# The first group's first part and the last group's last part as two halves in turn, with three written-out orders of steps

## The chip, the cores and the metric

One kernel runs on one core of a Trainium2 chip. The metric is the device time of one execution in microseconds, as a median of several runs. The core has a matrix engine (TensorE, PE in the profile; PEld is its weight load), a vector engine (VectorE, DVE), an activation engine (ScalarE, ACT), GpSimd (POOL), and SyncE (SP), whose queue issues nearly all transfers here. Each engine takes its own instructions strictly in the order in which the program lists them, and waits on semaphores for what others make.

## The reference

The input x is 64 batches of 256 tokens with 256 features, all in float32. Two layers are applied, each a graph-attention block (gnn) and a feed-forward block (ffn), each behind a layernorm and added to x:

```python
x = x + gnn0(layernorm(x))   # relu(x W1+b); attention without mask; relu(. W2+b); attention with mask
x = x + ffn0(layernorm(x))   # top 127 of 256 tokens go through gelu(. w1 + b1) w2 + b2, scaled
x = x + gnn1(layernorm(x))   # one masked attention
x = x + ffn1(layernorm(x))   # a Mamba-2 block: causal conv of 4 taps, decay matrices per head, gate
def attention(inp, mask, W, a):
    h = inp @ W
    e = leaky_relu((h @ a1)[:, :, None] + (h @ a2)[:, None, :])
    return elu(softmax(where(mask, e, -inf)) @ h)
```

Every batch is worked alone: no number passes from one batch to another.

## The kernel before, in words

The 64 batches are taken in 32 groups of two (`G = 2` at L46). A group is 512 token columns (`T`) or 4 chunks of 128 tokens (`C`). Each group passes three parts, which are Python generators: `first_part` (gnn0, L489 to L569), `middle` (ffn0 and gnn1, L571 to L724) and `last` (ffn1, L726 to L932, then the store at L972). A `yield` ends a step, and a step is a handful of instructions. First part has 55 steps, middle 57, last 87. Here they are lanes a, b and c; c30.12 is step 12 (from 0) of the last part of group 30.

The order in which all engines get their instructions is written out by hand. `along` (L234) reads the 199 letters of `ORDER` (L22 to L25) again and again; a letter runs one step of its lane, a capital also lets the lane begin its next group. A lane that has nothing to do is skipped. So in the steady round the first part of one group runs beside the middle part of the one or two groups before it and the last part of the group before those. At the beginning b and c have no work, at the end a has none, then b has none. a0 runs alone up to step 54, a1 alone up to step 34 (then b0 begins), and c31, the last part of the last group, runs all of its 87 steps alone.

What the steps do, as far as it matters below:

- a (gnn0): steps 1 and 2 layernorm; 3 and 4 transposes on PE; 5 to 8 the products with `mlp1_w`; 9 to 12 products with `W_fc` and two folded columns; 13 to 16 `scores` (transposes into `fb`, max, leaky relu, exp with sums on ACT, the division on POOL, L446); 17 to 20 the rest of `W_fc`; 21, 22 `turned`; 23 to 34 `u` and the two nested elu (ACT, DVE, ACT, DVE, POOL L541); then `mlp2_w`, `W_hand` and a second attention.
- b (ffn0, gnn1): 3 to 7 the choice of tokens; 8 to 27 four products `ph` with a gelu each; 28 to 35 `py` with `w2`; 36 to 42 the sum, moments and layernorm; 43, 44 the score columns (DVE, `junk` L689); 45 `fb` on PE; 46 to 56 attention.
- c (ffn1): 1 to 4 layernorm, transposes, `pd`; 5, 6 the step sizes and their running sum (`csT`, L753), stored to DRAM and spread back over the partitions by 8 DMAs (`E`, L781), one for each head; 8 to 31 five products `pp` with `W_in` (PE), each with the 4 conv taps (ACT L813, three DVE L817) and a silu (ACT L822, DVE L823), and for four heads `decays` (a minimum on DVE L792, four exp on ACT L798); 32 to 39 transposes `xd`; 40, 41 `pb` and `cb`; 42 to 73 per pair of heads `E * cb` (DVE L870), `pz` and gate, `py`, the sum (DVE L895) and gating (POOL L896); 74 to 86 the norm (`pss`, `pst`, L922) and four `po` with the sum into x, then the store.

Weights are made ready by two more generators: `made_ready_first` (L305) loads what a0 needs and folds the attention vectors into `W_fc` and `W_hand` (DVE, L311 to L318); `made_ready` (L341) loads everything else, folds `W_l1` (also L314), transposes the result (`pa`), halves some weights and multiplies `W_out` with `W_lin`. Its steps are taken in a0 after step 14, its DMAs are in the order of the list `fetches`, with many small ones (`dtb`, `negA`) ahead of the attention vector `a_l1` (L347).

Of the kernel before, what the change touches and what calls it, by code (L numbers as in the profile page):

```python
# [8 lines left out]
F32 = mybir.dt.float32  # L9
# [10 lines left out]
GELU_A = 0.044715  # L20
ORDER = (
    "cAaccbbbbacbaabccccabbcaccbaccabcbcbacbbcaaaccacaabaaaabccccccccacccacccabcabaaccabccccaccccacababcc"  # L22
    "ccbbccccabcccacaccccbcacbcBbcacbacbbacaaacbacbaabcbbacbcbbbcbbccaCbcbbbcabaaacacbacbaabbbcabbbbbccc"
# [4 lines left out]
def kernel(ctx: ExitStack, tc: tile.TileContext, a: dict, out: bass.AP):  # L28
# [16 lines left out]
    G = 2  # L45
    T = G * N  # L46
    C = T // P
# [6 lines left out]
    assert N == 256 and D == 256 and DS == 64 and HD == 64 and B % G == 0  # L54
# [10 lines left out]
    def view(ap, g):  # L65
        return ap[g * G : (g + 1) * G].rearrange("b (h p) d -> p (b h) d", p=P)

    xin = ctx.enter_context(tc.tile_pool(name="xin", bufs=6))
    first_x = xin.tile([P, C, D], F32, tag="xt", name="xt")
    nc.sync.dma_start(first_x, view(x, 0))  # L70
# [39 lines left out]
    neghalf = cons("neghalf", P, C)  # L110
# [64 lines left out]
    W_in = rows("W_in", a["L1_ffn_W_in"])  # L175
    conv_w = cons("conv_w", P, KC, 4)
    fetched((conv_w, a["L1_ffn_conv_w"].rearrange("(k p) t -> p k t", p=P)))
    conv_b = column("conv_b", a["L1_ffn_conv_b"])

    dtb = cons("dtb", 32 * G, 1)  # L180
    negA = cons("negA", 32 * G, 1)
    for t, ap in ((dtb, a["L1_ffn_dt_bias"]), (negA, a["L1_ffn_A_log"])):
        fetched(*((t[q * NH : (q + 1) * NH, :], ap.unsqueeze(1)) for q in range(32 * G // NH)))
# [42 lines left out]

    def mm(to, lhsT, rhs, start, stop):
        nc.tensor.matmul(to, lhsT, rhs, start=start, stop=stop)  # L228
# [4 lines left out]

    def along(parts, order, n):  # L234

        at = [0] * len(parts)
        now = [None] * len(parts)  # L240
        while at[-1] < n:
            for letter in order:
                i = "abc".index(letter.lower())
                if at[i] == n:
                    continue
                if now[i] is None:
                    if letter.islower() or not (at[i - 1] > at[i] if i else at[0] - at[-1] < 5):
                        continue
                    now[i] = parts[i](at[i])
                if next(now[i], True):  # L250
                    at[i] += 1
                    now[i] = None
# [8 lines left out]
    def power(to, of, scale, eps):  # L261

        nc.gpsimd.tensor_scalar(to, of, scale, eps, ALU.mult, ALU.add)
        nc.gpsimd.tensor_tensor(to, to, neghalf, ALU.pow)

    def moments(xt, s):

        st = sm(f"st{s}", P, C, 6, bufs=1)
        mv = sm(f"mv{s}", P, C, 2, bufs=2)
        rstd = sm(f"rstd{s}", P, C, bufs=2)  # L270
        for c in range(C):
            nc.vector.bn_stats(st[:, c, :], xt[:, c, :])  # L272
        for c in range(C):
            nc.vector.bn_aggr(mv[:, c, :], st[:, c, :])
        power(rstd, mv[:, :, 1], 1.0, EPS)
        return mv, rstd

    def layernorm(xt, mv, rstd, tag):

        xn = [t512(tag, "xn") for _ in range(G)]  # L280
        for c in range(C):
            if c % 2 == 0:
                yield
            nc.vector.tensor_scalar(
                chunk(xn, c), xt[:, c, :], mv[:, c, 0:1], rstd[:, c : c + 1], ALU.subtract, ALU.mult
            )
        return xn
# [3 lines left out]

    def transposed(xn, take):

        xT = []
        for k in range(KD):
            yield
            pt = psum("pt")
            for c in range(C):
                tr(pt[:, tok(c)], chunk(xn, c)[:, k * P : (k + 1) * P], ident)
            xT.append(take())  # L300
            nc.scalar.copy(xT[k], pt)  # L301
        return xT
# [17 lines left out]
    def made_ready_first():  # L320
# [13 lines left out]
        folded(W_fc, avs, H1, t512("w", "junk"))  # L334
        folded(W_hand, hands, D, t512("w", "junk"))
# [4 lines left out]

    def made_ready():  # L341

        fetch()
# [10 lines left out]
        nc.sync.dma_start(W_lin, a["L1_ffn_W_lin"].rearrange("(k p) n -> p k n", p=P))  # L354
        yield
# [15 lines left out]

        for t in (b1h, conv_w, conv_b, W_in[:, :, :DI]):
            nc.vector.tensor_scalar(t, t, 0.5, None, ALU.mult)
# [21 lines left out]
    def scores(f1, f2, mask, strict, tag):  # L395

        yield  # L400
        fb = psum("fb")
        for c in range(C):
            tr(fb[:, tok(c)], f2(c).to_broadcast([P, P]), ident)
        halves = [slice(h * N, (h + 1) * N) for h in range(2)]
        es = [t512(tag, "e") for b in range(G)]
        rows = [fb[:, b * N : (b + 1) * N] for b in range(G)]
        top = sm("top", P, C)
        if mask is None:
            most = sm("most", P, G)
            nc.vector.tensor_reduce(most, fb.rearrange("p (b j) -> p b j", b=G), AX.X, ALU.max)  # L410
            for c in range(C):
                nc.vector.tensor_scalar(
                    top[:, c : c + 1], most[:, c // 2 : c // 2 + 1], f1(c), -1.0, ALU.add, ALU.mult
                )
        else:
            most = sm("topm", P, C)
            for c in range(C):
                e = es[c // 2][:, halves[c % 2]]
                nc.vector.tensor_tensor_reduce(
                    e, rows[c // 2], mask[:, c % 2, :], 1.0, -3e38, ALU.add, ALU.max, most[:, c : c + 1]  # L420
                )
            for c in range(C):
                nc.vector.tensor_scalar(
                    top[:, c : c + 1], most[:, c : c + 1], f1(c), -1.0, ALU.add, ALU.mult
                )
        yield
        nm = sm("nm", P, C)
        nc.vector.scalar_tensor_tensor(nm, top, ALPHA, top, ALU.mult, ALU.min)  # L428
        den = sm("den", P, C)
        for c in range(C):  # L430
            e = es[c // 2][:, halves[c % 2]]
            nc.scalar.activation(e, rows[c // 2] if mask is None else e, AF.Prelu, bias=f1(c), alpha=ALPHA)  # L432
        yield
        for c in range(C):
            e = es[c // 2][:, halves[c % 2]]
            nc.scalar.activation(e, e, AF.Exp, bias=nm[:, c : c + 1], accum_out=den[:, c : c + 1])  # L436
        yield
        if strict:

            nc.vector.scalar_tensor_tensor(den, nm, 1e30, den, ALU.is_lt, ALU.mult)  # L440
        nc.vector.reciprocal(den, den)
        if strict:
            nc.vector.scalar_tensor_tensor(den, nm, 1e30, den, ALU.is_lt, ALU.mult)
        for c in range(C):
            e = es[c // 2][:, halves[c % 2]]
            nc.gpsimd.tensor_scalar(e, e, den[:, c : c + 1], 1.0, ALU.mult, ALU.mult)  # L446
        return es

    def turned(es, tag):

        res = []
        for e in es:
            yield
            pt = psum("pt")
            for h in range(2):
                for j in range(2):
                    tr(
                        pt[:, j * N + h * P : j * N + (h + 1) * P],
                        e[:, h * N + j * P : h * N + (j + 1) * P], ident,
                    )  # L460
            at = t512(tag, "at")
            nc.scalar.copy(at, pt)  # L462
            res.append(at)
        return res

    def elu2(u):

        w = t512("w", "w")
        nc.scalar.activation(w, u, AF.Exp)
        yield  # L470
        nc.vector.tensor_scalar(w, w, 1.0, None, ALU.min)
        nc.scalar.activation(w, w, AF.Exp, bias=neg1)
        yield
        nc.vector.scalar_tensor_tensor(w, w, -1.0, u, ALU.add, ALU.max)  # L474
        return w

    def project(xT, w, tag):

        res = []
        for c in range(C):  # L480
            yield
            pp = psum("pp")
            for k in range(KD):
                mm(pp[:, : D + 2], xT(k, c), w[:, k, :], start=(k == 0), stop=(k == KD - 1))
            h = tiled(t2, (P, D + 2), tag, "hp", 4)
            nc.scalar.copy(h, pp[:, : D + 2])
            res.append(h)
        return res

    def aggregate(at, h, i):  # L490

        u = psum("u")
        for half in range(2):
            for j in range(2):
                mm(
                    u[:, half * D : (half + 1) * D],
                    at[i][:, j * N + half * P : j * N + (half + 1) * P],
                    h[2 * i + j][:, :D],
                    start=(j == 0), stop=(j == 1),
                )  # L500
        return u
# [69 lines left out]
    def ffn0(xt, of):  # L571
# [17 lines left out]
        for c in range(C):  # L589
            b, h = c // 2, c % 2  # L590
            if c == 2:
                yield
# [418 lines left out]
```

## Time and profile before

| | |
|---|---|
| time, median of 3 runs | 3716.49 us (3714.97 to 3717.17) |
| the profiled execution's own time | 3714.94 us |
| its span from the first to the last instruction | 3713.2 us |
| PE busy | 3546.0 us (95%) |
| DVE busy | 2843.1 us (77%) |
| ACT busy | 2170.8 us (58%) |
| POOL busy | 1084.3 us (29%) |
| mean granted TensorE clock | 0.982 |
| store of group 0 issued | 363.64 us |
| stores of groups 27, 28, 29, 30, 31 issued | 3330.49, 3440.34, 3540.87, 3625.36, 3709.05 us |

The stores are one steady round, 109.85 us, apart up to group 28. Busy time is an average over stages with different limits; the table by windows below splits it. In such a table each row is a stretch of the span, followed by its length and the busy time and count of each engine, the granted clock of TensorE (PEclk), and the share and rate of DMA. A table of waits tells which engine's instruction waited for what, in total, how often, and the longest.

### The profile page before, as it was taken

To read this page: it belongs to the slowest core of one execution; us is meant where nothing else is said; L and a number is where in the kernel's file an instruction comes from. 1 tells how busy PE (TensorE), PEld (TensorE's weight loads), DVE (VectorE), ACT (ScalarE), POOL (GpSimd) and SP (SyncE) were. 2 spreads that over 40 slices of the span, in tenths; PEclk is the share of its full clock that TensorE was granted. 3 is DMA by queue.
4 is the path that set the end of the run, shared out by engine and by line. 5 is a ranking of instruction groups with operands and counts; after the bars stand their busy time and mean duration, and the time that the engine had idled before them with its cause. 6 is when DMAs were issued, how large, how long until landed. Compare 5 with 4: busy or idle time off the path is not lost.

```text
span 3713.2 us, 50288 instructions
## 1 busy us (share of the span) xinstructions
PE 3546.0 (95%) x16924; PEld 2545.1 (69%) x16924; DVE 2843.1 (77%) x7209; ACT 2170.8 (58%) x4901; POOL 1084.3 (29%) x1261
## 2 busy tenths in 40 slices
PE   6899999999999999999999999999999999999775
PEld 4567677777767777767777776776776777776553
DVE  3467877778788778787777788877878777778875
ACT  3456565566566556656656656656666655665443
POOL 1123222233332233332223333223333223332221
PEclk8899999999999999999999999999999999999887
DMA  3000111110111111011111011111001111101111
GB/s 114 1 33 16 42 48 48 39 48 15 42 48 48 39 48 38 25 42 48 48 39 48 15 42 48 48 39 48 30 33 42 48 44 43 48 15 37 42 42 47
DMA packets 89074, 150.87 MB, mean 41 GB/s; under 512 B 12144, under 2 KB 55024, under 8 KB 88816
## 3 DMA queue, kind: packets, MB, share of 16 engines
q1 hardware_dynamic: 88816, 147.65, 12.2%
q8 instruction: 135, 2.21, 0.2%
q14 instruction: 123, 1.01, 0.1%
HBM read 125.86 MB, written 17.56 MB: 39 GB/s over the span
## 4 chain that ended last, share of the span: by engine, by line
PE 69%; DVE 16%; ACT 9%; issue 3%; POOL 2%; DMA 1%; SPq 0%; ACTq 0%; POOLq 0%; DVEq 0%
PE pp L228 30%; PE u L228 9%; PE py L228 9%; PE pz L228 6%; PE pt L231 4%; PE pa L228 3%; PE po L228 3%; DVE g L645 3%; ACT e L436 2%; ACT g L646 2%; DVE st L272 1%; ACT e L432 1%; PE fb L231 1%; DVE xt L569 1%; ACT v L637 1%
## 5 line engine op out<-in xcount | busy, mean ns | idle before, releaser
L798 ACT ACTIVATE E<-E,ncs 128x256 f32<-128x256 f32 (+1 forms) x1024 | 381.4, 445 | 159.9 <-DVE E L792 146.9
L446 POOL TENSOR_SCALAR e<-e,den 128x256 f32<-128x256 f32 x384 | 194.6, 523 | 929.0 <-DVE nm L428 415.6
L228 PE MATMUL pp<-W_fc,o 128*128 128x256 f32 (+1 forms) x2048 | 461.2, 380 | 0.0
L228 PEld LDWEIGHTS pp<-W_fc,o 128*128 128x128 f32 x2048 | 383.6, 190 | 67.2 <-issue 15.3
L817 DVE SCALAR_TENSOR_TENSOR xs<-pp,conv_w,xs 128x510 f32<-128x510 f32 (+2 forms) x480 | 357.1, 744 | 54.2 <-ACT xs L813 42.9
L822 ACT ACTIVATE th<-xs 128x512 f32<-128x512 f32 x160 | 100.8, 630 | 357.2 <-DVE xs L817 345.2
L228 PE MATMUL pp<-xT,W_in 128*128 128x512 f32 x640 | 299.9, 601 | 0.0
L541 POOL TENSOR_TENSOR o<-w,o 128x512 f32<-128x512 f32 x128 | 167.5, 1309 | 316.0 <-DVE w L474 316.0
L228 PE MATMUL py<-w,g 128*128 128x256 f32 x1024 | 237.3, 385 | 21.0 <-DVE g L648 21.0
L228 PE MATMUL u<-at,h 128*128 128x256 f32 x1024 | 247.1, 385 | 0.5 <-ACT at L462 0.5
L228 PE MATMUL pp<-o,mlp_w 128*128 128x512 f32 x512 | 238.5, 608 | 5.7 <-POOL o L541 5.7
L228 PE MATMUL pz<-xT,W_in 128*128 128x512 f32 x512 | 243.7, 599 | 0.0
L228 PE MATMUL po<-W_ol,xs 128*128 128x256 f32 x1024 | 243.3, 382 | 0.0
L792 DVE TENSOR_TENSOR E<-E,ccs 128x512 f32<-128x512 f32 x256 | 243.2, 970 | 0.0
L228 PE MATMUL ph<-sel,w 128*128 128x256 f32 x1024 | 242.1, 380 | 0.5 <-ACT sel L615 0.5
L228 PE MATMUL pp<-xT,mlp_w 128*128 128x512 f32 x512 | 241.4, 596 | 0.2 <-ACT xT L301 0.2
L228 PEld LDWEIGHTS py<-w,g 128*128 128x128 f32 x1024 | 191.7, 192 | 70.4 <-DVE g L648 46.3
L870 DVE TENSOR_TENSOR E<-E,cb 128x768 f32<-128x768 f32 x256 | 236.1, 962 | 1.1
L896 POOL TENSOR_TENSOR xs<-xs,gz 128x512 f32<-128x512 f32 x128 | 194.5, 1519 | 132.3 <-DVE xs L895 132.3
L272 DVE BATCH_NORM_STATS2 st<-xt 128x6 f32<-128x256 f32 x512 | 185.2, 414 | 59.0 <-POOL xt L724 32.0
L228 PEld LDWEIGHTS u<-at,h 128*128 128x128 f32 x1024 | 189.8, 190 | 58.7 <-issue 30.7
L679 POOL TENSOR_TENSOR xt<-xn,xt 128x512 f32<-128x512 f32 x64 | 81.2, 1269 | 508.0 <-DVE xn L676 508.0
(178 smaller groups left out, 7666.2 us busy)
## 6 DMA issues: line engine op xcount, KB each, us to landing
E<-csd SPq DMA_DIRECT2D x256, 384.0 KB
xt<-in_x_dram SPq DMA_DIRECT2D x32, 512.0 KB
out_dram<-xt SPq DMA_DIRECT2D x32, 512.0 KB
cs<-xs SPq DMA_DIRECT2D x64, 64.0 KB
w<-in_L_ffn_w_dram SPq DMA_DIRECT2D x2, 1024.0 KB
W_in<-in_L_ffn_W_in_dram SPq DMA_DIRECT2D x1, 1160.0 KB
mlp_w<-in_L_gnn_mlp_w_dram SPq DMA_DIRECT2D x2, 512.0 KB
W_fc<-in_L_gnn_W_fc_dram SPq DMA_DIRECT2D x2, 512.0 KB
```

Of the source, the lines that this page charges most:

```text
L228: nc.tensor.matmul(to, lhsT, rhs, start=start, stop=stop)
L231: nc.tensor.transpose(to, of, eye)
L272: nc.vector.bn_stats(st[:, c, :], xt[:, c, :])
L446: nc.gpsimd.tensor_scalar(e, e, den[:, c : c + 1], 1.0, ALU.mult, ALU.mult)
L541: nc.gpsimd.tensor_tensor(o1[m], w, o1[m], ALU.add)
L645: nc.vector.tensor_tensor(g, g, v, ALU.mult)
L792: nc.vector.tensor_tensor(diag, diag, ccs[:, :, :, h : h + 1].to_broadcast([P, G, 2, P]), ALU.min)
L798: nc.scalar.activation(e[:, b, to], e[:, b, to], AF.Exp, bias=ncs[:, b, half, h : h + 1])
L817: nc.vector.scalar_tensor_tensor(s3[:, :, d:], p3[:, :, : N - d], conv_w[:, m, 3 - d : 4 - d], s3[:, :, d:], ALU.mult, ALU.add)
L822: nc.scalar.activation(th, s, AF.Tanh)
L870: nc.vector.tensor_tensor(e2, e2, cb2, ALU.mult)
L896: nc.gpsimd.tensor_tensor(yt, yt, gz, ALU.mult)
```

## The change

**Sizes.** The functions of the three parts move into a function `sized(G, own)`, made three times: once for groups of two batches, and once for each half of one group (one batch, `G = 1`, 256 token columns). A half has its own instructions on half the columns; tiles that a group has once are shared by the two halves, each using its columns (`wide`, `columns`). For one batch the first part has 42 steps of the same kinds, the last part 78.

**Lanes.** Group 0's first part is lane a (half 0) and lane d (half 1). Group 31's last part is lanes e and f. Lane w makes the weights ready, in 13 steps, with one order of loads: group 1's x now comes ahead of all weights; `a_l1`, `W_out` and `W_lin` come ahead of the small ones (`conv_w`, `dtb`, `negA` and so on). x of group 0 is loaded and the last group stored by halves.

**Orders.** `FIRST` (305 letters) is run once, then `ORDER` (199 letters, a new one) until lane a has done all groups (29 times), then `LAST` (403 letters) once, then the lanes in turn until all is done. Decoded step by step, with the rules of `is_there`:

- `FIRST` begins d0 w0 d1 d2 a0 d3 a1 d4 w1, and the halves go on in turn. a1 (group 1) begins as letter 86, when half 1 has five steps left, and b0 begins as letter 97, at a1.6. At the end of `FIRST` the next steps of the lanes are a3.0, b1.31 and c0.10. The order before passes the same point (there a3.0, b1.31 and c0.11 are next).
- The new round has the same lanes in the same phase as the old, with steps moved by up to some ten places.
- `LAST`: lane b ends its last group just before c30.75 (c30.74 before). e and f may not begin before that, so of their 156 letters only 15 take effect: f does steps 0 to 7 and e 0 to 6 beside c30.76 to c30.86. All the rest of the two halves is run by the closing loop, one step of each in strict turn. Of group 31's middle part only steps 0 to 6 now lie beside c29's end (15 before), and its gelu stage (8 to 27) lies beside c30.4 to c30.25 (before: ahead of c30.7).

Two smaller edits: the row of sums `ss` uses the buffer of `cs` (tag c8) in place of one of four of tag m, and the moments have three buffers in place of two.

```diff
-    first_x = xin.tile([P, C, D], F32, tag="xt", name="xt")
-    nc.sync.dma_start(first_x, view(x, 0))
+    first_x = xin.tile([P, 4, D], F32, tag="xt", name="xt")
+    for half in range(2):
+        nc.sync.dma_start(batch(first_x, half), view(x, 0, half))
...
-    def made_ready_first():
+    def made_ready():
...
-    def made_ready():
-
-        fetch()
+        yield
+        fetch(third_ones - second_ones)
         a_l1 = t512("xd", "a_l1")
...
         nc.sync.dma_start(W_lin, a["L1_ffn_W_lin"].rearrange("(k p) n -> p k n", p=P))
+        fetch()
...
+    def sized(G, own=None):
+        taken = {}
+        def wide(make, tag, *rest):
+            if own is None:
+                return make(tag, *rest)
+            i = taken[tag] = taken.get(tag, -1) + 1
+            if i == len(shared.setdefault(tag, [])):
+                shared[tag].append(make(tag, *rest))
+            return shared[tag][i]
+        def columns(tag, name, most=512):
+            t = wide(lambda tag, name: t512(tag, name) if most == 512 else tiled(t2, (P, most), tag, name, 4), tag, name)
+            return t[:, (own or 0) * N : (own or 0) * N + T]
...
-        ss = t512("m", "ss")
+            ss = columns("c8", "ss")
...
+    both, one = sized(2), [sized(1, half) for half in range(2)]
...
+    def first_half(half):
+        xt = batch(first_x, half)
+        moments = one[half]["moments"](xt, 0)
+        loaded(1)
+        yield from one[half]["gnn0"](xt, moments, lambda: early(1))
+        if at["a"] + at["d"]:
+            of[1, 0] = both["moments"](first_x, 1)
...
+    def last_half(half):
+        xt = batch(xts[n - 1], half)
+        mv, rstd = of[2, n - 1]
+        yield from one[half]["ffn1"](xt, (batch(mv, half), batch(rstd, half)))
+        nc.sync.dma_start(view(out, n - 1, half), xt)
...
+    def is_there(lane):
+        return {
+            "a": at["a"] - at["c"] < 5,
+            "b": at["a"] > at["b"] and at["d"],
+            "c": at["b"] > at["c"],
+        }.get(lane, lane in "dw" or at["b"] == n)
...
     with tc.manual_schedule():
-        along((first_part, middle, last), ORDER, n)
+        for lane in FIRST:
+            step(lane, True)
+        while at["a"] < n:
+            for letter in ORDER:
+                step(letter.lower(), letter.isupper())
+        for lane in LAST:
+            step(lane, True)
+        while any(at[lane] < TIMES[lane] for lane in LANES):
+            for lane in LANES:
+                step(lane, True)
```

## The prediction

> **What bounds the kernel now.** I read the page's 40 slices first, to see where the work is thin.
>
> ```profile
> PE   6899999999999999999999999999999999999775
> ...
> PEclk8899999999999999999999999999999999999887
> ```
>
> PE is full except in the first two slices and the last three. Next the windows, cut where the lanes change: two of the start, the middle, six of the end, one round.
>
> ```profile
> 0.00:101.35 101.35, 59.26 (x229) 41.76 (x229) 34.76 (x140) 30.18 (x65) 15.01 (x30) 0.85 0.34 104
> 101.35:275.70 174.35, 156.40 (x657) 115.01 (x658) 87.67 (x269) 82.92 (x183) 42.02 (x54) 0.94 0.04 12
> ...
> 3457.80:3491.00 33.20, 17.05 (x60) 11.31 (x60) 27.94 (x75) 12.28 (x26) 3.75 (x4) 0.74 0.20 67
> ...
> 3551.70:3584.60 32.90, 17.28 (x57) 10.27 (x56) 26.61 (x63) 12.44 (x24) 3.90 (x5) 0.77 0.23 77
> 3584.60:3616.00 31.40, 29.66 (x149) 18.93 (x149) 27.36 (x49) 18.57 (x46) 10.97 (x10) 0.92 0.08 26
> 3616.00:3633.90 17.90, 11.69 (x58) 8.21 (x56) 6.77 (x20) 3.77 (x6) 4.77 (x5) 0.91 0.09 30
> 3633.90:3692.30 58.40, 32.70 (x111) 16.18 (x110) 37.14 (x51) 21.99 (x48) 4.96 (x3) 0.74 0.18 57
> ...
> 1682.34:1792.17 109.83, 108.94 (x530) 78.65 (x529) 88.04 (x223) 67.51 (x154) 33.77 (x40) 1.00 0.12 40
> ```
>
> A round is PE-bound: 108.94 of 109.83 us. In the start no engine is full; in the end DVE (third pair) and PE take turns. Last, PE's waits, before 276 us and (second fence) after 3457 us.
>
> ```profile
> PE pa L231 <- DVE junk L314: 18.7, 1, 18.7
> PE pt L231 <- DVE xn L284: 14.8, 2, 8.4
> PE pt L231 <- POOL e L446: 6.7, 3, 5.3
> ```
>
> ```profile
> PE pt L231 <- DVE xs L823: 30.2, 6, 6.2
> PE fb L231 <- DVE junk L689: 22.6, 2, 11.4
> ```
>
> Between 276 and 3457 only two are left: py for g (15.4 us, 28 times) and pd for xT (10.0, 29 times), 0.9 us a round.
>
> [...]0.74 and 0.77 in the two stretches with 11 us gaps, 1.00 in the round. [...]424 ns for 256 columns (L689), 691 for 512 (L823); from PSUM 478 (L676), 745 (L895).[...]
>
> **Halving on PE** costs nothing: eight records of 256 columns (u at 3602.35 in the chain) take 1.73 us, four of 512 (pz at 3604.08) 1.72.
>
> **The start**, to the end of FIRST, old 275.7 us. PE's work to there, from the spacing of starts in a round (first part 46, middle 26, last 37, sum 109 as the window has it): three first parts 138, b0 26, 31 steps of b1 12.5, c0's 10 steps 4.5, weights 5: 186. The first product stands at 10.5, so the old loss is 275.7 - 10.5 - 186 = 79.
> - Goes: 18.7. `pa` stood in PE's queue in the middle of a0 and waited for `a_l1`, issued at 34.79 because SP spent 22.4 to 32.3 on dtb and negA, and landed at 44.57. Now it is issued some 12 us earlier, and `pa` (w5) stands behind a0.38, near 60. The small loads are due at w6, in a1.
> - Goes: 6.4 of the 14.8 (a1 waiting behind a0's end; the other 8.4 is the time to the first instruction). b0 fills from a1.6, not from a1.35.
> - New: group 1's 512 KB ahead of the weights, +1.8 us at the 286 GB/s of the first 20 us. `W_fc` and `av` landed at 10.99, and DVE folded to 17.98, 7 us; now near 20, while PE has 6.9 us of mlp1 from some 11 on: 2 lost (0 to 4). Queued behind the fold on DVE: only the scores, due later.
> - Stays: the elu chain. ACT has 8 x 2 x 0.45 (L637: 461 ns) = 7.2 against PE 6.9, and a tail through POOL: 2. The second scores of a and d: chain 5.3, PE's fill 3.5 and 2.7: 5. Clock: 4.
> - From a1 on: old 174.35 for some 139 of work, 35 lost; with b0 beside all of a1 I leave 20 (12 to 30). This is judged, not counted.
>
> Losses 2 + 2 + 5 + 4 + 20 = 33; the phase ends at 10.5 + 186 + 33 = 230: **-45** (-28 to -58).
>
> **The round, 29 times.** Both old waits keep their neighbours. py waits since b26's product (DVE 1697.65) stands behind a54's moments; a54 again stands right before b26, and PE's fill from b28 to c12 is the same. pd and the copy it waits for are one step. New margin: from c46 to c56 (py to py) PE has 2 x 0.44 + 2 x 1.73 + 1.72 = 6.1 us of work (old 7.8); DVE needs 0.75 + 4 x 0.97 + 0.49 = 5.1, hidden with 1.0 left. Before c32, 1.7 us of `junk` moved behind what it needs: safer. `ss` in cs's buffer: cs is read 36 steps earlier; nothing. **0** (-6 to +10: 0.2 a round won, 0.35 lost).
>
> **The end**, from c29.12 (3457.8) to 3713.2, 255.4 us.
> - c29.12 to c29.40, 33.2 with DVE at 84%: the order hardly changes. **-1** (-3 to 0).
> - To c30's store, from c29.74 near 3517, 108. Three pieces. (i) To c30.9, old 34.7: b31's gelu and `py` leave it; the choice's chain and PE work of 18 remain: 22. (ii) Conv, old 32.9: `ph` and `py` come in, PE 20.5 in place of 14.3, while b31's moments and junk leave; DVE has conv 15.2, min 4.6, gelu 6.1, y 0.9 = 26.8, and waits for ACT: 30. (iii) The rest, old 40.4: what left (ii) lands here, DVE 29.8 + 9.6 = 39.4 before the last po, so 42 + 9, less 2 that overlap: 49. Sum 101: **-7** (-15 to +2). The fb wait loses its cost: `fb` now stands behind c30.45, not ahead of the xd transposes.
> - c31's head. From 3625.4 to 3633.9 one chain (xn, pt, pd, dz, csT) runs alone, 8.5 us. As f0 to f7 it lies beside c30's norm and po; its 2.9 us on PE falls partly into waits there (pss, pst: 2.0). What is late next is c30's own po. **-8.5** (-10 to -4). On SP, the halves' four small stores stand ahead of c30's store, which nobody waits for; 12 half E loads in place of 6, some 6 us of issuing, still wait for c30's last py and are due at the first min, over 6 us later.
> - The tail, old 79.3. Conv: the period of one product with a head's decays is 6.58 (3663.26 - 3656.68). In lockstep DVE does 6 taps of 0.52 (pitch 0.785, less 255 x 1.04 ns), twice 0.35 and twice 0.4, 4.6; then it waits for e's exp and f's scaling on ACT, 0.75 + 0.5 and latency, and for tanh: 6.5. **No gain.** E stage: period 7.04 (3683.92 - 3676.88); DVE in halves 5.9 to 6.2, and py of one half hides behind E of the other: 2 x 0.9 and 2 x 0.9 for the later pairs, 3.5. Norm and store: POOL 1.27 to 0.7, sq, pss and ss halved, half a store: 2.5. **-6** (-12 to +4[...]).
>
> Sum -22.5, **-22** (-8 to -38).
>
> **Sum.** -45 + 0 - 22 = -67. The profiled execution took 3714.94 (span 3713.2 and 1.74 around it): 3648. The median of the runs is 1.55 above it: **3649**.
>
> **Rivals.**
> 1. *The ends pack better* (0.17). If DVE reaches 88% in the end, its 174 us there and 9 for halving need 208 of 255, -47; the start could lose 15, not 33. About two thirds of the way, -39 and -57: 3620. For: waits of 11 us in both b/c stretches. Against: in lockstep DVE stands behind ACT.
> 2. *The end gives nothing* (0.20). The halves share tiles; where one half's write must wait for the other's use, lockstep is serial, or the 9.6 us of DVE that land in (iii) cost what the head frees. End 0, start -38: 3678. For: DVE is at 87% in 3584.6 to 3616. Against: each half has its own columns.
> 3. *Slower* (0.05). The py margin: if DVE reaches E late in each round, PE waits in all 29. It decides from 67 / 29 = 2.3 us a round; at 2.9 (DVE 3.9 us later than counted) +84: 3733. For: the margin shrinks by 1.7. Against: no such wait exists now.
> 4. *It doesn't do what it says* (0.03). Shared tiles make the halves serial at both ends and the gaps stay: within 0.2%.
>
> The likeliest case has the remaining 0.55, with 3627 to 3672 as its own range.
>
> **Numbers.** Measurement can tell about 0.2%, 7.4 us, from no change. The range takes in most of 1 and 2: 3612 to 3684. Faster 0.92 (likeliest, 1, 2), same 0.03 (4), slower 0.05 (3).
>
> **What would show it.** PE's wait for L314 is gone. Group 0's store is issued near 319 (363.64 - 45); stores stay 109.85 apart; from c30's store to the end there are 73 us (87.8 - 8.5 - 6); the conv period in the tail is 6.5. I am wrong in the start if group 0's store comes before 306 or after 336, in the round if its period leaves 109.6 to 110.2, in the end if c30's store to the end takes under 66 or over 84.

## The result and the profile after

| | before | after |
|---|---|---|
| median of the runs | 3715.95 us (3714.97 to 3717.17) | 3654.07 us (3652.69 to 3655.5) |
| ratio, 95% interval | | 0.9833 (0.9816 to 0.985) |
| span of the profiled execution | 3713.2 us | 3652.1 us |
| mean granted TensorE clock | 0.982 | 0.990 |
| store of group 0 issued | 363.64 us | 319.89 us |
| stores of groups 28, 30 issued | 3440.34, 3625.36 us | 3392.44, 3586.13 us |

The change takes 61.9 us off the time and 61.1 off the span. The stores split it. Up to group 0's store it is 43.75 us. From there to group 28's it is 4.15 (28 rounds of 109.73 us in place of 109.88). From group 28's store to the end it is 13.2 (259.66 us in place of 272.86).

The page's slices of the kernel after: the first two are now nearly full, and the last three have 8, 7 and 6 tenths in place of 7, 7 and 5.

```profile
PE   8999999999999999999999999999999999999876
...
PEclk9999999999999999999999999999999999999989
```

The windows of after, cut at the same events as those of before in the next fence (columns: stretch, its length, busy us and count of PE, PEld, DVE, ACT, POOL, the granted clock, DMA's share and rate). First the start, up to a1's first transposes, and (after only) from there to the end of `FIRST`. Then two pieces of the last part of group 30: its convolution, from the first `pp` to `pb`, and from there to its last `py`. Then the head of group 31's last part (to its first `pp`), its convolution to the last run of `xd` transposes (the first three stand single before it, one at each new tile), and its E stage to `pss`.

```profile
0.00:66.75 66.75, 53.86 (x233) 42.39 (x233) 31.06 (x132) 30.62 (x76) 15.73 (x35) 0.97 0.51 158
66.75:231.33 164.58, 154.36 (x686) 115.33 (x685) 94.52 (x290) 85.31 (x187) 41.86 (x55) 0.98 0.06 18
...
3491.36:3528.73 37.37, 30.66 (x101) 19.52 (x100) 25.24 (x41) 19.68 (x40) 1.97 (x4) 0.83 0.20 68
3528.73:3564.82 36.09, 26.51 (x126) 15.72 (x125) 29.93 (x72) 14.42 (x37) 12.53 (x12) 0.81 0.06 22
3564.82:3585.59 20.77, 16.86 (x78) 10.53 (x77) 10.93 (x30) 10.16 (x17) 8.42 (x9) 1.00 0.00 1
3585.59:3613.54 27.95, 10.18 (x45) 8.02 (x44) 20.50 (x53) 14.44 (x33) 0.00 (x0) 0.75 0.34 109
3613.54:3637.34 23.80, 20.20 (x118) 14.97 (x118) 22.94 (x48) 11.71 (x34) 4.92 (x6) 0.93 0.10 33
...
```

The same stretches of the kernel before:

```profile
0.00:101.35 101.35, 59.26 (x229) 41.76 (x229) 34.76 (x140) 30.18 (x65) 15.01 (x30) 0.85 0.34 104
...
3551.64:3587.54 35.90, 20.28 (x70) 12.94 (x68) 29.52 (x77) 14.53 (x29) 3.96 (x5) 0.74 0.21 71
3587.54:3612.45 24.91, 24.47 (x130) 15.77 (x129) 22.02 (x30) 15.29 (x40) 8.36 (x8) 0.96 0.09 33
3612.45:3633.91 21.46, 13.94 (x66) 8.76 (x65) 9.20 (x25) 5.03 (x9) 7.38 (x7) 0.92 0.07 25
3633.91:3667.07 33.16, 11.86 (x24) 4.87 (x23) 16.90 (x27) 12.34 (x23) 0.00 (x0) 0.65 0.24 76
3667.07:3694.81 27.74, 22.24 (x101) 12.41 (x101) 21.79 (x26) 11.17 (x27) 5.10 (x3) 0.86 0.10 29
...
```

Read row against row, group 30's convolution has become 1.5 us longer and what follows 11.2. The piece ahead of them (from c29's last `py` on, by the same views 35.70 us before and 24.43 after) gives -11.3, so that together 1.4 are lost. The head gives -0.7; in the changed kernel a product of lane b (`u`, 1.99 us) now stands behind c30's last `py`, and so in the head. The tail's convolution gives -5.2, its E stage -3.9, and norm and store, which come last (18.39 and 14.76), -3.6: -12.8 for the tail (unrounded).

PE's waits of after, first those before 228 us, then those after 3400:

```profile
PE pt L254 <- DVE xn L405: 6.8, 1, 6.8
PE pt L254 <- POOL e L473: 3.8, 4, 2.7
```

```profile
PE pt L254 <- DVE xs L851: 24.1, 6, 5.9
PE fb L254 <- DVE junk L715: 14.2, 2, 7.6
```

The 18.7 us for the fold of `W_l1` are gone. What is left in the start is the way to the first instruction, 6.8 us. At the end the wait of `fb` has gone down from 22.6 to 14.2 us only.

### The profile page after: what moved, and what is told of

Its sections match the earlier page's. It is cut to its first block, busy times and chain, and to the rows that moved or that the text cites. A ratio compares the mean times of both kernels' runs of the same rounds, so it can differ in the third digit from the quotient of the medians.

```text
span 3652.1 us, 50662 instructions
## 1 busy us (share of the span) xinstructions
PE 3533.4 (97%) x17004; PEld 2550.6 (70%) x17004; DVE 2842.1 (78%) x7275; ACT 2189.1 (60%) x4942; POOL 1146.8 (31%) x1274
## 4 chain that ended last, share of the span: by engine, by line
PE 81%; DVE 12%; ACT 4%; issue 1%; POOL 1%; DMA 1%; SPq 0%; ACTq 0%; POOLq 0%; DVEq 0%
PE pp L251 31%; PE u L251 10%; PE py L251 9%; PE po L251 7%; PE pz L251 6%; PE pt L254 5%; PE ph L251 4%; PE pa L251 3%; PE psel L251 2%; DVE st L393 1%; DVE xt L595 1%; DVE g L674 1%; DVE w L498 1%; DVE g L671 1%; DVE w L594 1%; PE pss L251 1%
## 5 line engine op out<-in xcount | busy, mean ns | idle before, releaser
L845 DVE SCALAR_TENSOR_TENSOR xs<-pp,conv_w,xs 128x510 f32<-128x510 f32 (+5 forms) x495 | 359.9, 728 | 93.9 <-ACT xs L841 79.9
L251 PE MATMUL pp<-xT,W_in 128*128 128x512 f32 (+1 forms) x660 | 303.6, 593 | 0.0
L850 ACT ACTIVATE th<-xs 128x512 f32<-128x512 f32 (+1 forms) x165 | 101.7, 617 | 326.6 <-DVE xs L845 311.4
L925 POOL TENSOR_TENSOR xs<-xs,gz 128x512 f32<-128x512 f32 (+1 forms) x132 | 205.9, 1561 | 203.0 <-DVE xs L924 200.5
L899 DVE TENSOR_TENSOR E<-E,cb 128x768 f32<-128x768 f32 (+1 forms) x264 | 250.5, 964 | 1.1
L251 PE MATMUL pz<-xT,W_in 128*128 128x512 f32 (+1 forms) x528 | 242.8, 583 | 0.0
L567 POOL TENSOR_TENSOR o<-w,o 128x512 f32<-128x512 f32 (+1 forms) x132 | 180.7, 1369 | 197.8 <-DVE w L501 197.8
L251 PE MATMUL pp<-xT,mlp_w 128*128 128x512 f32 (+1 forms) x528 | 236.5, 583 | 0.7 <-ACT xT L419 0.7
L251 PE MATMUL pp<-o,mlp_w 128*128 128x512 f32 (+1 forms) x528 | 231.1, 590 | 2.9 <-POOL o L567 2.9
L820 DVE TENSOR_TENSOR E<-E,ccs 128x512 f32<-128x512 f32 (+1 forms) x264 | 224.3, 863 | 0.0
```

The source lines that it names most:

```text
L567: nc.gpsimd.tensor_tensor(o1[m], w, o1[m], ALU.add)
L820: nc.vector.tensor_tensor(diag, diag, ccs[:, :, :, h : h + 1].to_broadcast([P, G, 2, P]), ALU.min)
L845: nc.vector.scalar_tensor_tensor(s3[:, :, d:], p3[:, :, : N - d], conv_w[:, m, 3 - d : 4 - d], s3[:, :, d:], ALU.mult, ALU.add)
L850: nc.scalar.activation(th, s, AF.Tanh)
L899: nc.vector.tensor_tensor(e2, e2, cb2, ALU.mult)
L925: nc.gpsimd.tensor_tensor(yt, yt, gz, ALU.mult)
```

## The experiments

Times are medians; "span" is that of the profiled execution. The changed kernel has 3654.07 and 3652.1. In the edits, lines of an order are cut to their beginnings.

### e1: the old round in the new kernel

```diff
 ORDER = (
-    "cAaaccbbbbbbacabaccccbccaabacccabcbccabaacbcca...
+    "cAaccbbbbacbaabccccabbcaccbaccabcbcbacbbcaaacc...
```

> The changed kernel with the order of the round of before; start and end as changed. Theory: a round is 0.12 us longer (109.85 in place of 109.73, PE's wait in pd at 0.34 in place of 0.19), so 29 rounds give +3.5: about 3657.5 us. Rival, the round is the same and the 4 us between the stores of groups 0 and 28 come from the place of the store in the round: 3654, unchanged.

Measured: 3660.62, span 3657.0. The stores are 109.89 us apart again. So the new order of the round is worth 4.9 us of span and 6.6 of median, some 4 by the stores' distance. (By the stores, e1's start is 1.7 us shorter than the changed kernel's, its 28 rounds are 4.3 longer and its end is 2.4 longer.) Here are PE's waits in the rounds beside that of `py` for g (15.5 and 15.7 us), of e1 and of the changed kernel:

```profile
PE pd L251 <- ACT xT L419: 9.8, 28, 0.3
```

```profile
PE pst L254 <- ACT ss L944: 5.9, 29, 0.2
PE pd L251 <- ACT xT L419: 5.5, 29, 0.2
```

The wait of `pd` has nearly halved and a new one at `pst` takes more than that: 25.3 us of waits in e1, 27.1 in the changed kernel. So the gain isn't in a wait. Between 300 and 3380 us PE is busy 3054.8 us for 14803 records in e1 and 3053.1 for 14827 in the changed kernel, which is 0.2 us less in each round. Where it comes from shows in single records. Nearly all records of a kind have one length in both kernels; a few are longer (here those of `u`: least, middle and greatest ns, e1 first):

```profile
L251 PE MATMUL u<-at,h x896: 379/379/483, 374.9 to 3363.0; 128*128 128x256 f32 x180
```

```profile
L251 PE MATMUL u<-at,h x896: 379/379/382, 375.8 to 3354.6; 128*128 128x256 f32 x180
```

The long ones of `u`, two in a round, stand directly behind `py<-E,xd`, whose first operand has 64 columns where theirs has 128. Read record by record, every product in that place is 104 or 105 ns longer, and so is one directly behind `pss` (32 columns); a transpose there moves what follows by 57 ns behind `py` (166 in place of 109) and by 51 behind `pss` (160). In the new order transposes stand in two such places in which the old one has products. That makes 0.10 us a round, two thirds of the gain of 0.15. It is read from the two traces; no run tests it alone.

### e2: the old end

```diff
 LAST = (
-    "ececefefceecbbceccbbcbffbbbccfcbbfceccebbfccc...
+    "cccbbbbcbbccccbbcccbccbcbcbcbbccccbbccccccccc...
-    TIMES = {"a": n, "b": n, "c": n - 1, "d": 1, "e": 1, "f": 1, "w": 1}
+    TIMES = {"a": n, "b": n, "c": n, "d": 1, "e": 0, "f": 0, "w": 1}
```

> The changed kernel with the end of before: the order of before from c29.10 on, group 31's last part whole and alone. Theory: start and end add up, so the end's share comes back, 255.4 less 242.9 us = +12.5: about 3666.5 us. Rival, half the end's share was a shift from the round: 3660.

Measured: 3667.87, span 3662.5: 13.8 more in the median, 10.4 in the span. Start and end add up, and the 13.2 us that the stores give to the end lie between the two.

### e3: the last group whole, but begun early

The 87 steps of the whole group begin as lane f beside c30.75; lane e is gone and `LAST` has its letters changed for that.

```diff
-        "e": lambda g: last_half(0),
-        "f": lambda g: last_half(1),
+        "f": lambda g: last(n - 1),
```

> Group 31's last part whole, but begun beside c30.75 in the places where the halves began; everything else as changed. It parts the earlier begin from the halving. Theory from the two traces: the earlier begin is worth some 2 to 3 us and the tail in halves 12.8, so without halves about +12: 3665. Rival, the prediction's own split (begin 8.5, tail 6): +6, 3660.

Measured: 3661.88, span 3659.6, between the two. Halving is worth 7.5 us of span, the early beginning with the same pairing of b and c about 5 (e2 less e3, with e4's 2.4 for the pairing). The convolution's period is 6.58 here as before. My prediction had it the other way round: 8.5 for the beginning, 6 for the halves. Here is e3's tail, cut like the rows above: convolution, E stage, norm and store.

```profile
3583.90:3615.19 31.29, 10.15 (x24) 4.15 (x23) 17.28 (x28) 12.33 (x23) 0.00 (x0) 0.69 0.29 97
3615.19:3642.97 27.78, 22.10 (x101) 12.45 (x101) 21.78 (x26) 11.17 (x27) 5.08 (x3) 0.86 0.10 29
3642.97:3659.60 16.63, 9.67 (x45) 6.68 (x44) 2.86 (x6) 1.22 (x2) 2.46 (x3) 1.00 0.09 33
```

It is 75.70 us long, where the kernel before has 79.29 and the changed one 66.51. So 9.2 of the tail's 12.8 us are the halves' own; where the other 3.6 come from is said below.

### e4: the old pairing of b and c, with the halves

From c30.75 on, where e and f begin, the order is as in the changed kernel.

```diff
 LAST = (
-    "ececefefceecbbceccbbcbffbbbccfcbbfceccebbfccc...
+    "cccbbbbcbbccccbbcccbccbcbcbcbbccccbbccccccccc...
```

> The changed kernel with the order of before for b30, c29, b31, c30 from c29.10 to c30.75, and the halves after that as changed. Theory: the stretch from c29's last py to c30's last py takes 99.7 us in the new order and 96.5 in the old, so the old pairing is 3 us better: 3651. Rival, the prediction's step that the new pairing wins 7 there and something else loses: 3661.

Measured: 3654.05, span 3649.7. The median says nothing, the span, which is that of the fastest of the four runs, 2.4 us less. The stores put it in its place: from group 28's to group 30's there are 191.51 us in e4 and 193.69 in the changed kernel. In no reading does the new pairing of lanes b and c at the end win anything, and the rival of 3661, which was my prediction's -7, falls.

### e5: group 0 whole

The whole group's 55 steps are lane a, with the weight steps at their places and lane d gone.

```diff
 FIRST = (
-    "dwddadadwaaadawdaaddadaddaaaaadddaaddaaaaddad...
+    "awaawaawaaaaaaaaaaaaaaaaaaaaaaaaaaaaaawawaaaa...
-        "a": lambda g: first_part(g) if g else first_half(0),
+        "a": lambda g: first_part(g) if g else first_whole(),
```

> The changed kernel with group 0's first part whole (55 steps of lane a), the loads and the lane that makes the weights ready in the same places as changed, and groups 1 and later in the changed order. It parts halving at the start from the moved weights and from b0's earlier begin. Theory: the moved pa step gives 18.7 us and b0's begin some 15, halving gives the rest of 44: about +10, 3664. Rival, halving gives nearly all of the first 34.6 us: +25 or more, 3680.

Measured: 3666.8, span 3662.1, group 0's store at 329.60. So halving group 0 is worth 9.7 us there. Where it shows, in PE's waits of e5 up to 276 us (against 6.8 and 3.8 above):

```profile
PE pt L253 <- DVE xn L404: 13.4, 2, 7.2
PE pt L253 <- POOL e L472: 8.7, 3, 5.3
```

### e6: the kernel before with its weight steps later

The steps of `made_ready` are taken in a0 after step 38 in place of 14. Nothing else is changed.

```diff
-            if i > 14:
+            if i > 38:
```

> The kernel before with one number changed: the steps that make the weights ready are taken in a0 after step 38, not after step 14; loads in the old order. Theory: the 18.7 us wait of PE on a_l1 goes, and what waited next (the first attention's division, 5.3, and xn) stays: 3716 - 18 = 3698. Rival, the wait only moves (DVE then folds while the score chain waits): 3710 or more.

Measured: 3691.98, a ratio of 0.9939 (0.9924 to 0.9954), span 3690.3: 22.9 us less than before with one number changed. Group 0's store is at 341.02, 22.6 earlier than before. That is more than the wait of 18.7, behind which work of PE that was ready stood too: the products with `W_fc` that are listed after `pa` begin at 46.75 before and at 26.96 in e6. PE's waits of e6 up to 276 us show one reason (6.7 us before, in the prediction's fence):

```profile
PE pt L231 <- POOL e L446: 2.7, 3, 1.3
```

The longest wait for the second scores' division was 5.3 us; now the weights' transposes and products stand in it. The other reason is the clock: up to a1's first transposes, which come at 79.06 in place of 101.35, it is 0.95 in e6 and 0.85 before. The four records of `pa` show the difference (before, behind the long wait, then e6):

```profile
45.08 1.88 PE L231 MATMUL pa<-ident,columns 128*128 128x128 f32 x4 [18.65 <-DVE junk L314]
```

```profile
58.04 0.60 PE L231 MATMUL pa<-ident,columns 128*128 128x128 f32 x4
```

With e5 the start splits into the place of the weight steps (363.64 to 341.02, 22.6), the rest of `FIRST` and the loads (to 329.60, 11.4) and the halves (to 319.89, 9.7).

### e7: the old order of loads

```diff
-        fetch(third_ones - second_ones)
+        fetch()
```

> The changed kernel with the small loads (conv_w, dtb, negA and so on) ahead of a_l1, W_out and W_lin on SP's queue again. Theory: pa stands near 62 us and a_l1 lands before 45 even so, so the order of the loads gives nothing: 3654. Rival, the prediction's words that both the earlier load and the later step matter: a_l1 is late for w4's fold on DVE, +2 to +10.

Measured: 3653.84, span 3654.1. Loading `a_l1` ahead of the small ones gives nothing that shows. So of the two it is the place of `pa` in PE's order that counts.

### e8: the two halves half a period apart

The letters of e and f for the convolution of group 31 are written out, so that one half's three taps stand beside the other's silu, min and exp. The end of the order is shown.

```diff
+    "ccbccccbccbccccbbcccccccccbcbcccbcbcfeccfffcfecfeccefcececccfefeefeffefeffefffeefeefefffeefeefefffee"
+    "feefeffeefeffeeee"
```

> The changed kernel with half 0 half a period behind half 1 in the conv stage of the tail, in place of strict turns. In strict turns DVE waits 1.68 us a period for exp of both halves and the scaling on ACT, all in a row. Theory: one half's taps then cover the other's exp and scaling, period 5.1 to 5.5 in place of 6.26, four periods: -3 to -4.6, 3650. Rival, ACT's order makes other waits of the same length: 3654.

Measured: 3653.92, span 3652.1. The period fell from 6.26 to 4.93 us, further than the theory says (5.1 to 5.5), and the last run of `xd` transposes began at 3608.71 in place of 3613.54. The time stayed. PE's order of time shows where it went (start, duration, operation, in brackets the idle time before it). The changed kernel, then e8:

```profile
3613.54 3.04 PE L254 MATMUL pt<-ident,xs 128*128 128x128 f32 x13 [5.79 <-DVE xs L851]
3616.51 1.70 PE L251 MATMUL pb<-cs,xs 64*128 64x256 f32 x8
3618.14 1.99 PE L251 MATMUL pz<-xT,W_in 128*128 128x256 f32 x8
```

```profile
3608.71 1.97 PE L253 MATMUL pt<-ident,xs 128*128 128x128 f32 x8 [4.45 <-DVE xs L850]
3612.18 1.33 PE L253 MATMUL pt<-ident,xs 128*128 128x128 f32 x5 [1.50 <-DVE xs L850]
3613.44 2.92 PE L250 MATMUL pb<-cs,xs 64*128 64x256 f32 x8
3616.29 3.78 PE L250 MATMUL pz<-xT,W_in 128*128 128x256 f32 x8
```

The same 8 records of `pb` take 2.92 in place of 1.70, those of `pz` 3.78 in place of 1.99, and `py` begins at 3620.00 in place of 3620.06. From the first line of transposes here to `py` the granted clock is 0.50 in e8 and 0.75 in the changed kernel. In both, the transposes are slow behind the idle time: 0.23 us each behind 5.79 us in the changed kernel, 0.25 behind 4.45 in e8. In the changed kernel PE then works without a break and is fast after 3.0 us. In e8 its work begins earlier but is broken by another wait, of 1.50, and it is slow for 11.3 us. Neither story of the expectation had this; e10 tests it.

### e10: e8 with PE kept at work

One product that nothing reads follows each silu of a half but the first.

```diff
                 xs[m] = s
+                if G == 1 and m != KI:
+                    mm(psum("warm"), xs[m - 1 if m else KI][:, :P], W_in[:, 0, :512], True, True)
```

> The staggered halves, and after each silu of a half but the first one product of PE that nothing reads (128 by 512 columns of W_in), eight in all, so that TensorE's records do not thin out in the convolution of group 31. The outputs are not touched; the extra products are work that the changed kernel does not have. Theory, that the stagger's 3 us were lost again because PE came out of the convolution at a slow clock: pb and pz return to 1.7 and 2.0 us in the first pairs, the convolution's period stays near 4.9, the time is 3650 to 3651, 3 us under the changed kernel. Rival, that what follows is set by another engine: pb and pz get faster and the time stays 3654. Third case: the extra products stand in the way of pp, the period goes back over 5.5 and the time is 3654 to 3657.

Measured: 3651.07 (3650.46 to 3652.54), span 3649.4. In the order of time:

```profile
3612.50 1.83 PE L250 MATMUL pb<-cs,xs 64*128 64x256 f32 x8
3614.26 3.37 PE L250 MATMUL pz<-xT,W_in 128*128 128x256 f32 x8
3617.56 1.52 PE L250 MATMUL py<-E,xd 128*64 128x256 f32 x16
```

The transposes (the last five in 0.76 us, 1.33 in e8) and `pb` (1.83, 2.92 in e8) are fast again, `py` begins 2.5 us earlier, and the span is 2.7 shorter. So the slow clock did eat the stagger's gain. What the extra products would give with the halves in strict turns was not run. One number of the expectation missed: `pz` still takes 3.37 (the clock is 0.79 from the transposes at 3609.36 to `py`, 1.00 in the convolution; e8 has 0.50 and 0.82). Why it dips once more was not followed.

### e11: e10 with the old pairing of e4

```diff
 LAST = (
-    "ccccbbcccbbcbbbbcccbbcccbbcccbccbcbcbcccccccc...
+    "cccbbbbcbbccccbbcccbccbcbcbcbbccccbbccccccccc...
```

> The same extra products and the stagger, with the order of lanes b and c from the kernel before at the end. If the old pairing is worth the 2.4 us that its span showed (its median showed none) and this adds to the extra products' 3, 3648; if the old pairing is worth nothing, the same time as the staggered kernel with the extra products, 3650 to 3651; if neither gives anything, 3654.

Measured: 3649.47 (3647.84 to 3651.07), a ratio of 0.9821 (0.9808 to 0.9835), span 3647.7. This is the fastest version, 4.6 us under the changed kernel, and all of its runs lie below all of that one's, though the intervals of the two ratios overlap. The old pairing gives 1.7 us of span here, 2.4 in e4: about 2, at the edge of what the times can tell. From group 28's store to group 30's there are 193.69 us in e10 and 191.51 here, the same two numbers as in the changed kernel and e4.

## Why the prediction was right, and where it was not

3649 was predicted and 3654.07 measured: the sum of -67 should have been -62. It was right by its largest term. The parts were not all right: the end lacks 9 us, and the total is only 5 off because the round gave 4 that nobody had foreseen. That part is luck.

**The start, -45, measured -43.75.** `pa` stands at 61.9 us (near 60 was said), and its wait is gone. The 1.8 us for group 1's 512 KB ahead of the weights was 2.1 (`av` landed at 13.07). The elu chain lost 2.3 (2). The fold of `W_fc` held PE for 0.4 only (2), the second scores for some 2.5 (5). The term that was judged, 15 us less lost from a1 on, came out: `FIRST` ends at 231.33 (230 was said), and from a1's first transposes on PE is idle for 10.2 us of 164.58 at a clock of 0.98, where the prediction's fence has 18.0 of 174.35 at 0.94. Priced by the round's spacing of starts, which is an estimate, the loss there fell from 30 to 16. The 4 us for the clock were an estimate that no run tests alone: up to a1's first transposes the clock is 0.97 (0.85 before). Two things were missed. Moving the weight steps is worth 22.6 and not 18.7, since they fill the wait for the second scores (2.7 us in place of 6.7) and the clock is higher (0.95 in place of 0.85, e6). And the earlier issue of `a_l1`, which I named beside the place of `pa`, adds nothing: in e7 the small loads stand ahead of it again at no cost.

**The round, 0, measured -4.** It lies in the range of -6 to +10. The step that failed is "pd and the copy it waits for are one step" as a reason for no change: `pd`'s wait went from 10.0 to 5.5 us. But waits don't carry the gain (e1). I looked for it only among waits, and two thirds of it lie in PE's records, in what a product directly behind a narrower one costs (104 ns).

**The end, -22, measured -13.** Three of its terms are off, in both directions.

- *To c30's store, "Sum 101: -7".* By the windows, whose cuts differ from the prediction's, the pieces up to c30's last `py` sum to +1.4, and e4 says the pairing wins nothing. Piece (i) went nearly as said, -11.3 for -12.7. Piece (ii) was said to lose 3 with DVE as the bound and 6.2 us more on PE (20.5 for 14.3). It grew by 1.5, with 10.4 more on PE: 30.66 of 37.37 us, at a clock of 0.83. I had put the work that moves in at the round's prices into a stretch whose clock I had just read as 0.77. At those prices the work in it grew by 7.9 by these cuts (an estimate from the spacing of starts), so that by this estimate the slow clock makes 2.5 of the 10.4; how much of the stretch's length that is, no run tells. Piece (iii) was said to grow by 8.6. It grew by 11.2 to c30's last `py`, and by 19.6 to c30's store, where the prediction's piece ends, because c31's head now lies in it. The time that I had left for its waits was too short. And "the fb wait loses its cost" was wrong. `fb` is behind c30.45 as said, but what it waits for moved with it. Here are the waits in PE's order of time in that piece, of the changed kernel:

```profile
3538.16 1.78 PE L254 MATMUL fb<-ident,f 128*128 128x128 f32 x4 [6.59 <-DVE junk L715]
...
3548.82 1.15 PE L254 MATMUL pt<-ident,e 128*128 128x128 f32 x4 [2.99 <-POOL e L473]
```

- *c31's head, "-8.5".* The head itself lies beside c30's norm, but the gap between c30's last `py` and c31's first `pp` shrank by 0.7 only (by 2.4 in e4, where no product of lane b stands behind that `py`). The step that failed is "its 2.9 us on PE falls partly into waits there". In the order of time of the changed kernel the waits of `pss` and `pst` are over before f's first transposes, at 3573.01 (the `pss` records begin at 3568.01). From there PE has work of both, and the head's part of it, the next `pd` too, pushes c30's `po`:

```profile
3571.29 0.65 PE L254 MATMUL pst<-ident,ss 128*128 128x128 f32 x4 [0.68 <-ACT ss L944]
3573.01 0.87 PE L254 MATMUL pt<-ident,xn 128*128 128x128 f32 x4 [1.06 <-DVE xn L405]
...
3575.10 1.99 PE L251 MATMUL po<-W_ol,xs 128*128 128x256 f32 x8
```

- *The tail, "-6", measured -12.8.* The mechanism was right, the sizes were not, and 3.6 us of it are not the halves' (e3). Of these, 1.8 are in norm and store: the same instructions, whole, take 18.39 before at a clock of 0.89, and 16.63 in e3 at 1.00. Some 1.9 are in the convolution: before, PE comes out of waits of 3.75 and 0.56 us and takes 3.74 for the first four records of `pp` (10.61 for all 20); in e3 it comes straight from c30's `po` and takes 8.75 for the 20, and ACT has the first `pp` 1.9 us after its start in place of 3.8. ACT's first steps, before (`pp` begins at 3633.91) and in e3 (at 3583.90):

```profile
3637.69 0.78 ACT L813 ACTIVATE xs<-pp,conv_b,conv_w 128x512 f32<-128x512 f32 x1 [5.79 <-PE pp L228]
```

```profile
3585.82 0.78 ACT L840 ACTIVATE xs<-pp,conv_b,conv_w 128x512 f32<-128x512 f32 x1 [7.35 <-PE pp L250]
```

 What is left is the halves' 9.2. For the convolution I had "no gain"; it is 3.3. The period is 6.26 and not 6.5: DVE takes the six taps in 2.94 us where 3.12 was worked out. The taps of one half do stand 0.52 apart, but the first of the other half follows after 0.40. Before and in e3 the period was 6.58: that is 0.32 a period, 1.0 in three. The other 2.4 come from the first two products, ahead of the first decays, which I hadn't priced apart: 11.5 us in e3 (13.5 before) became 9.2. There each half works while the other waits. DVE's order of time has a wait of 0.71 and one of 0.40 and then only 0.21, where e3 has 1.73, 2.04 and 0.76.

```profile
3587.36 2.94 DVE L845 SCALAR_TENSOR_TENSOR xs<-pp,conv_w,xs 128x255 f32<-128x255 f32 x6 [0.71 <-ACT xs L841]
3590.69 0.76 DVE L851 SCALAR_TENSOR_TENSOR xs<-th,xs 128x256 f32<-128x256 f32 x2 [0.40 <-ACT th L850]
...
3603.96 2.94 DVE L845 SCALAR_TENSOR_TENSOR xs<-pp,conv_w,xs 128x255 f32<-128x255 f32 x6 [1.68 <-ACT xs L841]
```

 The last line is of the steady period. Its wait of 1.68 for ACT, which has the exp of both halves ahead of the scaling, is the cost of lockstep that the prediction named, and e8 takes it down to 0.65. The E stage's period is 5.69 (5.9 to 6.2 was said; 7.04 before), which gives 3.9 in place of 3.5. Norm and store give 1.9 by the halves, where 2.5 was said.

From c30's store to the end there are 65.97 us where 73 was said and "under 66" was named as the sign of an error: the 6.8 us by which the tail was underrated are that error. The head doesn't weigh there, since what it costs c30's `po` makes c30's store later too. Over the whole end, c30's pairing and the head, each some 8 us short, outweigh the tail.

Rival 1 (3620) had its price for full packing from DVE alone, with an estimate of 9 us for halving (in the tail DVE is busy for 46.19 us, 41.92 in e3, so 4.3 more); (ii) and (iii) show PE at clocks of 0.83 and 0.81 beside it. Rival 2 was nearer in its reason, that work moved out of one piece lands in the next, but the halves do run beside each other. The margin of rival 3 held: in the rounds no `py` waits for E, and the wait for g is 15.7 us in place of 15.4.

## What to carry to other kernels

A part that runs alone at the beginning or end, and is a chain over several engines, gained here from being cut into two independent halves (9.2 us in the tail) although each column became dearer (two taps of 255 columns take 1.03 us, one of 510 takes 0.785); price the stretches without other cover apart from the periodic ones, since there the halves hid most here (2.4 us in two products, 1.0 in three periods). Compare with a whole part that begins as early, or a faster PE is counted as the halves' gain (e3: 3.6 of the tail's 12.8 us). Before cutting anything, look for an instruction that stands in an engine's queue long before its result is due: here PE stood 18.65 us for `pa`, and half of the start's gain (22.6 of 43.75 us) came from taking the weight steps later. And where work is moved into a stretch in which TensorE is thin, price it at that stretch's clock (0.83 and 0.81 here), not at the round's (1.00).

## What the runs showed of the hardware that was not expected

- A stage that became shorter on DVE lost its gain on PE. In e8 the last run of `xd` transposes began 4.83 us earlier than in the changed kernel, `py` 0.06. The transposes took 0.23 us each behind an idle time of 5.79 us in the changed kernel, 0.25 and 0.27 behind 4.45 and 1.50 in e8, and 0.13 and 0.15 in e10, the latter behind an idle time of 1.52. In the changed kernel PE was fast after 3.0 us of work. In e8, after the wait of 1.50, it worked on without a break from 3612.18 and was slow up to 3620, 7.8 us; the cause of that difference is open. In the staggered kernel 16 product records that nobody reads brought back 2.7 us.
- DVE's taps of 255 columns stand 0.52 us apart where each needs what the one before wrote, and 0.40 where the next belongs to the other half. One dependent tap of 510 columns has a pitch of 0.785. Two dependent ones of half the size so take 1.03, 0.25 more than the whole one, and what the halves win lies in the waits between.
- A product of PE directly behind one with fewer columns in its first operand took 104 or 105 ns more than its kind, in the steady round and at a clock of 1.00: behind `py<-E,xd` (64) in e1 and in the changed kernel each time, behind `pss` (32) in e1. A transpose in that place cost 57 or 51 ns. So two orders can differ though their waits don't, here by 0.10 us a round.
